# Output product by half tiles in 32-token column tiles, with its queue neighbours in other steps

## The chip, the cores and the metric

One Trainium2 chip, and of it one core. Its engines run side by side, each with its own queue: PE (TensorE: matmuls, with PEld as its loads of weights), DVE (VectorE), ACT (ScalarE), POOL (GpSimd), and SP (SyncE), from which most transfers are issued. The metric is the time of one execution in device microseconds; the median of three executions is given, and lower is better.

## What is computed

Four blocks in a row, each added to `x` (4 batches, 1024 tokens, 256 channels): an attention to a context of 77 rows, a choice of experts, a second attention to that context with 16 heads, and a last attention of the tokens to themselves. Only the last one is touched. Its layer norm, its class of tokens and its output are, cut down:

```python
qkv = (x @ W_qkv).reshape(Bx, Nx, 3, H, D)           # 16 heads of 16
logits = jnp.einsum('bqhd,bkhd->bhqk', q * scale, k)
def masked_attn(tok_mask):                           # the 5 registers are always keys
    l = jnp.where(key_mask[:, None, None, :], logits, -jnp.inf)
    a = jax.nn.softmax(l, axis=-1)
    return jnp.einsum('bhqk,bkhd->bqhd', a, v)
x_pos, x_neg = masked_attn(pos), masked_attn(~pos)
reg_out = (x_pos[:, :REG] + x_neg[:, :REG]) * 0.5
tok_out = jnp.where(pos[:, :, None, None], x_pos[:, REG:], x_neg[:, REG:])
out = jnp.concatenate([reg_out, tok_out], axis=1).reshape(Bx, Nx, Cx) @ W_proj + b_proj
```

So each token attends to the keys of its own class and to the registers, and a register is the mean of two attentions. The output product with `W_proj` (256 x 256) follows, times a gate, added to `x`.

## The kernel before

Up to about 440 us the first three blocks run, in an order that a planner with costs and due times makes (`Plan`). They leave queries, keys and values in device memory (`q_d`, `k_d`, `v_d`). Nothing of that is touched.

The last block is one loop over steps k from -11 to 256 (lines 1902 to 1927). Sixteen steps are a unit: one batch b and four of its heads (u = 4b + g); four units, 64 steps, are a batch. Within a unit a step is one half of the queries (512) and one tile of 128 keys.

- `scores` (L1681): four matmuls of 64 x 128 by 512 columns, one for each head, and after each its exponential on ACT (L1692) into `p`.
- `maxima` (L1640): for a unit that is 11 steps ahead, four matmuls (L1649) and after each a maximum over 512 keys on DVE (L1656), interleaved with the scores head by head.
- `weigh` (L1696): for the step before, four column-tiled matmuls (L1702; 32 output rows for each head, the first of them the sum of the weights), a copy on ACT (L1716 or L1719) and a sum on POOL (L1720). At the end of a unit the sums and the results are laid out anew by transfers (L1726, L1730) into `sums` and `outs`.
- `maxima_end` (L1658) turns the maxima of half a unit (a minimum of negated values on DVE, L1663; a transpose, L1666; two DVE instructions, L1668 and L1669) and copies them by four transfers of 4 KB (L1672) into rows of the queries' tile, so that the scores come out with the maximum subtracted. Scores from step 16u + 8c on need the copies for (u, c).

All matmul outputs share 8 banks in turn (`bank`).

Other work is written as generators, and `plan` (L1859) says by hand in which steps a generator goes on: a number means after `weigh` of that step, a tuple means in the middle of the step (here behind the second head, L1915). The generators that the change touches, with k = 64b:

- `registers` (L1560): masked copies of the register queries on POOL; scores of all 16 heads' registers in four quarters of 256 keys, eight accumulating matmuls each (L1578), each quarter copied by ACT (L1586) in the middle of the next step into `p_r`, a tile that shares two buffers with the divisors; then a maximum, an exponential, transposes (L1600), the product with the values (L1607), and the result `reg_out`. Steps k+14 to k+31.
- `finish` (L1732): a batch's reciprocals (two halves, L1736), their store to device memory (L1738) and two broadcast loads of 512 KB as divisors (L1741), products on POOL (L1744), then for eight tiles of 128 tokens two matmuls by 256 columns (L1755) in one step, gate and sum on DVE (L1757) in the middle of the next, and for every second tile a transfer of `x` to the output. Steps k+67 to k+120, so beside the next batch; the last batch has `finish_unit` (L1766) and `first_heads` (L1783) for its first heads in place of it.
- `biased` (L1840) adds the bias on POOL, `unit` (L1846) loads queries and keys of a unit.

Who follows whom on PE, DVE, ACT and POOL in this loop is the order of the program. For SP it is not: the framework orders the transfers by a plan of its own, in which a transfer that is ready early can pass one that stands ahead of it in the program.

Of the kernel before, what the change touches and what calls it, by code (L numbers as in the profile page):

```python
# [10 lines left out]
F32 = mybir.dt.float32  # L11
# [8 lines left out]
P = 128  # L20
# [139 lines left out]
def block_kernel(ctx: ExitStack, tc: tile.TileContext, t_in: dict, out: bass.AP):  # L160
# [1399 lines left out]
    def registers(b):  # L1560

        qr = QR[b % 2]
        for g in range(G):
            for i in range(2):
                of_pair = qr[:, g, i, 32 * g : 32 * g + J * REG].rearrange("p (h i r) -> p h i r", h=2, i=2)
                q = of_pair[:, :, i, :]
                gp.tensor_tensor(q, bc(QT[(b * G + g) % SLOTS][:, i, 0:REG].bitcast(F32), 1, 2), rmul, ALU.mult)
                gp.tensor_tensor(q, q.bitcast(F32), radd, ALU.add)
            if g % 2:
                yield  # L1570

        p = work.tile([P, S], F32, name="p_r", tag="rinv", bufs=2)
        n = CH // 2
        for h in range(4):
            ps = bank("ps_rs", [P, n])
            for k in range(2 * G):
                g, i = divmod(k, 2)
                pe.matmul(  # L1578
                    ps,
                    qr[:, g, i, :],  # L1580
                    KT[(b * G + g) % SLOTS][:, i, h * n : h * n + n],
                    start=k == 0,
                    stop=k == 2 * G - 1,
                )
            yield
            se.copy(p[:, h * n : h * n + n], ps)  # L1586
            yield
        nm = work.tile([P, 1], F32, name="nm_r")
        ve.tensor_reduce(nm, p, AX.X, ALU.max, negate=True)
        yield  # L1590
        den = work.tile([P, 1], F32, name="den_r")
        se.activation(p, p, AF.Exp, bias=nm, accum_out=den)
        yield
        ve.reciprocal(den, den)
        pt = work.tile([P, T, P], F32, name="pt_r", tag="pt_r", bufs=1)
        for t4 in range(2):
            ps = bank("ps_rt", [P, T // 2, P])
            for i in range(T // 2):
                t = t4 * T // 2 + i
                pe.transpose(ps[:, i, :], p[:, t * P : t * P + P], ident)  # L1600
            se.copy(pt[:, t4 * T // 2 : (t4 + 1) * T // 2, :], ps)
            yield
        ps = bank("ps_ra", [P, J, D])
        for t in range(T):
            for g in range(G):
                r = slice(32 * g, 32 * g + 32)
                pe.matmul(  # L1607
                    ps[r],
                    pt[:, t, r],
                    V[b % 2][:, t, g * J : g * J + J, 1 : 1 + D],  # L1610
                    start=t == 0,
                    stop=t == T - 1,
                )
        mine = work.tile([P, J, D], F32, name="mine_r", bufs=1)
        ve.scalar_tensor_tensor(
            mine.rearrange("p j d -> p (j d)"),
            ps.rearrange("p j d -> p (j d)"),
            den,
            own.rearrange("p j d -> p (j d)"),
            ALU.mult,  # L1620
            ALU.mult,
        )
        yield
        ps = bank("ps_ro", [P, 2, REG])
        for g in range(G):
            at = 64 * (g % 2)
            pe.matmul(
                ps[at : at + 64, g // 2, :],
                mine.rearrange("p j d -> p (j d)"),
                half[:, g, :],  # L1630
                start=True,
                stop=True,
            )
        reg_out[b] = work.tile([P, 2, REG], F32, name="o_r")
        ve.tensor_copy(reg_out[b], ps)
        yield
# [21 lines left out]
    def maxima_end(u, c):  # L1658

        n = T // 2  # L1660
        nm = greatest.pop((u, c))
        least = last.tile([P, J, n], F32, name="nm1", bufs=2)
        ve.tensor_tensor(least, nm[:, :, :, 0], nm[:, :, :, 1], ALU.min)  # L1663
        yield
        ps = bank("ps_n", [J * n, P])
        pe.transpose(ps, least.rearrange("p j t -> p (j t)"), ident)  # L1666
        nmt = last.tile([J * n, 2, P], F32R, name="nmt", bufs=2)
        ve.tensor_copy(nmt[:, 0], ps)  # L1668
        ve.tensor_tensor(nmt[:, 1], ps, nmt[:, 0].bitcast(F32), ALU.subtract)  # L1669
        for i in range(2):  # L1670
            for k in range(2):
                nc.sync.dma_start(  # L1672
                    out=QT[u % SLOTS][k:P:64, i, c * CH : c * CH + CH].bitcast(F32),
                    in_=nmt[2 * n * i : 2 * n * (i + 1), k].bitcast(F32),
                )
        yield
# [55 lines left out]
    def finish(b):  # L1732
        o = outs.pop(b)
        for h in range(2):
            half_of = sums[b][:, h * P // 2 : (h + 1) * P // 2]
            ve.reciprocal(half_of, half_of)  # L1736
            yield
        nc.sync.dma_start(out=rinv_d[b].rearrange("h (t n) -> (h t) n", n=P), in_=sums[b])  # L1738
        rinv = [work.tile([P, S], F32, name="rinv", tag="rinv", bufs=2) for e in range(2)]
        for e in range(2):  # L1740
            nc.sync.dma_start(out=rinv[e], in_=bc(rinv_d[b][8 * e : 8 * e + 8], 1, D))  # L1741
        yield
        for e in range(2):
            gp.tensor_tensor(o[:, e, :], o[:, e, :], rinv[e], ALU.mult)  # L1744
            if e == 0:
                yield
        both = o[:, :, 0:REG]
        gp.tensor_scalar(both, both, 0.5, None, ALU.mult)
        gp.tensor_tensor(both, both, reg_out.pop(b), ALU.add)
        yield  # L1750
        x = X[b]
        for t in range(T):
            ps = bank("ps_o", [P, C])
            for e in range(2):
                pe.matmul(ps, o[:, e, t * P : t * P + P], w_proj[:, e, :], start=e == 0, stop=e == 1)  # L1755
            yield
            ve.scalar_tensor_tensor(x[:, t, :], ps, tg[:, 3:4], x[:, t, :], ALU.mult, ALU.add)  # L1757
            yield
            if t % 2:
                at = (t - 1) * P  # L1760
                nc.sync.dma_start(
                    out=out[b, at : at + 2 * P].rearrange("(t p) c -> p t c", p=P), in_=x[:, t - 1 : t + 1, :]
                )
            yield

    def finish_unit(g):  # L1766
        b = B - 1
# [15 lines left out]
    def first_heads():  # L1783
        x, o = X[B - 1], outs[B - 1]
        for t in range(T):
            ps = bank("ps_o", [P, C])
            pe.matmul(ps, o[:, 0, t * P : t * P + P], w_proj[:, 0, :], start=True, stop=True)
            yield
            ve.scalar_tensor_tensor(x[:, t, :], ps, tg[:, 3:4], x[:, t, :], ALU.mult, ALU.add)
            yield  # L1790
# [83 lines left out]
    for b in range(B):  # L1874
        k = 64 * b
        plan([k - 40, k - 38, k - 16, k - 14] if b else [-5, -4, -2, -1], fetch_values(b))
        scored = [filled(k + n) for n in (17, 19, 21, 23)]
        plan([k + 14, k + 15, *chain(*scored), k + 25, k + 26, k + 27, k + 29, k + 30, k + 31], registers(b))
        plan([k + 27, k + 28, k + 35, k + 36], biased(b))
        if b < B - 1:  # L1880
            tiles = chain(*([n, (n + 1,), n + 2] for n in range(k + 64 + 33, k + 64 + 55, 3)))
            plan([k + 67, k + 68, k + 74, k + 78, k + 80, *tiles], finish(b))
        else:
            plan([k + 19, k + 34], finish_unit(0))
            plan([k + 35, k + 39], finish_unit(1))
            plan(chain(*(filled(k + n) for n in (41, 42, 43, 45, 46, 47, 49, 50))), first_heads())
            plan([k + 51, k + 55], finish_unit(2))
    for u in range(1, NU):
        at = {1: -11, 2: -1}.get(u, 16 * u - (42 if u % G else 34))
        plan([at, at + 1, at + 2, at + 3], rows_ := unit(u))  # L1890
        plan({1: [-7, -6], 2: [3, 4]}.get(u, [at + 8, at + 9] if u % G else [at + 4, at + 5]), rows_)
    for u in range(NU):
        for c in range(2):
            at = 16 * u + 8 * c
            plan([at - 4, at - 3], maxima_end(u, c))
    end = 16 * NU
    mid = T // 2
    plan([end - 6, end - 4], divided(0, mid))
# [3 lines left out]
    for k in range(-LEAD, end + 1):  # L1902
# [7 lines left out]
        if um < NU:  # L1910
            for j in range(J):
                if attends:
                    scores(*now[:3], [j], now[3])
                maxima(um, km, [(j + 2) % J])
                if j == 1:  # L1915
                    for gen in middle.pop(k, []):
                        next(gen, None)
        elif attends:
            scores(*now[:3], range(2), now[3])
            for gen in middle.pop(k, []):  # L1920
                next(gen, None)
            scores(*now[:3], range(2, J), now[3])
        if before is not None:
            weigh(*before, um >= NU)
        before = now
# [89 lines left out]
```

## Time and profile before

| | us |
|---|---|
| median of the runs (1225.14 to 1228.18) | 1227.95 |
| the profiled execution, its own time | 1226.41 |
| its span in the trace | 1224.7 |
| first exponential of the loop | 466.8 |
| a unit without other work (599.4 to 639.2) | 39.8 |
| unit 5, with registers (681.8 to 738.6) | 56.8 |
| unit 6, with output tiles (738.6 to 784.6) | 46.0 |
| last maximum read by DVE starts (step 244) | 1187.8 |

The profile's rows name an engine, a line, what is written from what, and a shape. "x4" counts instructions merged in a row; "[0.81 <-PE ps_m L1649]" behind a row is idle time of the engine before it and what ended it. The ends of matmuls are modelled, so the time of a matmul is best read from the start of one to the start of the next. The granted clock of TensorE was 0.976 on average.

### The profile page before, as it was taken

The page shows a single profiled execution, that of the slowest core. Times are in us where ns is not written, and L with a number is a line of the kernel's source. Part 1 is how long each engine was busy: PE and PEld are TensorE (multiplying, and loading weights), DVE is VectorE, ACT ScalarE, POOL GpSimd, SP SyncE. Part 2 cuts the span into 40 slices and gives each one's busy share as a digit, 9 for nine tenths or more (in the row PEclk, how much of TensorE's full clock was granted, in tenths as well). Part 3 has the DMA queues.
Part 4 walks back from the last instruction along what each step waited for, and adds up shares of the span by engine and source line. Part 5 has one row for each costly group of instructions (what it writes and reads, how often), then busy time and mean ns, then how long its engine had stood idle before and what let it go on. Part 6 is the DMA issues. An engine that isn't in the chain of part 4 may idle for free.

```text
span 1224.7 us, 25560 instructions
## 1 busy us (share of the span) xinstructions
PE 1157.0 (94%) x9164; PEld 611.3 (50%) x9164; DVE 999.4 (82%) x2073; ACT 932.1 (76%) x1918; POOL 607.0 (50%) x682
## 2 busy tenths in 40 slices
PE   7999999999999899999999799999799999799898
PEld 5666776777777454344333344433344443244333
DVE  5898786776864489889999699999689899689884
ACT  4766567876566327899999698899699899689676
POOL 6454566667766532545443544343535334446431
PEclk9999999999999989999999899999899999899899
DMA  8000012111122865532334313334231452300011
GB/s 233 23 1 11 24 61 73 46 37 40 54 82 98 234 180 131 79 62 43 64 57 64 79 32 58 74 64 62 51 65 29 68 97 39 68 20 13 26 27 45
DMA packets 58149, 80.08 MB, mean 65 GB/s; under 512 B 15845, under 2 KB 41360, under 8 KB 58022
## 3 DMA queue, kind: packets, MB, share of 16 engines
q1 hardware_dynamic: 56262, 77.10, 28.2%
q8 instruction: 72, 1.18, 0.4%
q10 hardware_dynamic: 1248, 1.10, 0.3%
q0 software_dynamic: 512, 0.25, 0.2%
q14 instruction: 55, 0.45, 0.1%
HBM read 47.39 MB, written 26.07 MB: 60 GB/s over the span
## 4 chain that ended last, share of the span: by engine, by line
PE 75%; DVE 11%; DMA 5%; ACT 4%; POOL 2%; issue 1%; SPq 0%; ACTq 0%; DVEq 0%; POOLq 0%
PE av L1702 20%; PE sc L1684 18%; PE ps_m L1649 8%; DVE nm L1656 5%; PE ps_st L1121 4%; DMA slot<-nmt 3%; PE ps_av L1133 2%; PE ps_o L1199 2%; PE ps_o L1755 2%; PE ps_q L1234 2%; PE ps_xt L781 2%; PE ps_y L990 2%; PE ps_rs L1578 1%; ACT p L1692 1%; PE ps_xb L886 1%
## 5 line engine op out<-in xcount | busy, mean ns | idle before, releaser
L1656 DVE TENSOR_REDUCE nm<-ps_m 128x1 f32<-128x512 f32 x1024 | 627.8, 677 | 70.8 <-PE ps_m L1649 63.9
L1692 ACT ACTIVATE p<-sc 128x512 f32<-128x512 f32 x1024 | 544.1, 655 | 72.6 <-PE ps_m L1649 61.4
L1720 POOL TENSOR_TENSOR raw<-raw,part 128x512 f32<-128x512 f32 x213 | 272.7, 1281 | 376.7 <-ACT part L1719 365.9
L1649 PE MATMUL ps_m<-slot,slot 64*128 64x512 f32 x768 | 287.0, 458 | 0.9
L1702 PE MATMUL av<-p,v 128*32 128x512 f32 x2048 | 279.8, 614 | 1.2
L1684 PE MATMUL sc<-slot,slot 64*128 64x512 f32 x768 | 248.3, 440 | 29.8 <-DMA slot<-nmt 28.7
L1684 PEld LDWEIGHTS sc<-slot,slot 64*128 64x128 f32 x768 | 126.3, 188 | 183.3 <-ACT p L1692 59.2
L1719 ACT COPY part<-av 128x512 f32<-128x512 f32 x213 | 136.7, 642 | 24.3 <-PE av L1702 22.2
L1649 PEld LDWEIGHTS ps_m<-slot,slot 64*128 64x128 f32 x768 | 130.8, 188 | 39.5 <-ACT p L1692 23.6
L1280 POOL TENSOR_TENSOR ss_all<-ss_all,mhalf 128x16 f32<-128x16 f32 x32 | 92.6, 2903 | 12.8 <-DVE ss_all L1251 12.8
L1649 PE MATMUL ps_m<-kt,qt 64*128 64x512 f32 x256 | 91.6, 461 | 2.6 <-DVE stage L671 2.2
L1684 PE MATMUL sc<-qt,kt 64*128 64x512 f32 x256 | 87.8, 442 | 2.6 <-DMA qt<-nmt 1.2
L1702 PEld LDWEIGHTS av<-p,v 128*32 128x32 f32 x2048 | 41.5, 109 | 80.1 <-ACT p L1692 60.6
L1126 ACT ACTIVATE pt<-ps_st 77x512 f32<-77x512 f32 x128 | 64.2, 599 | 20.2 <-PE ps_st L1121 20.2
L1684 PEld LDWEIGHTS sc<-qt,kt 64*128 64x128 f32 x256 | 43.0, 186 | 67.7 <-DVE nm L1656 31.4
L1069 DVE TENSOR_REDUCE nm<-ps_e 128x4 f32<-128x308 f32 x128 | 51.7, 467 | 14.1 <-PE ps_e L1056 14.0
L769 ACT ACTIVATE xnp<-x,shift_all,rstd_all 128x256 f32<-128x256 f32 x96 | 52.0, 605 | 12.3 <-POOL shift_all L748 9.7
L736 DVE BATCH_NORM_STATS2 bn_st<-x 128x6 f32<-128x256 f32 x128 | 51.5, 402 | 2.3 <-DMA x<-in_x 1.8
L1649 PEld LDWEIGHTS ps_m<-kt,qt 64*128 64x128 f32 x256 | 41.5, 187 | 14.8 <-DVE nm L1656 3.4
L238 ACT COPY xt<-ps_xt 128x512 f32<-128x512 f32 (+1 forms) x57 | 31.7, 582 | 13.8 <-PE ps_xt L781 13.3
L746 POOL TENSOR_TENSOR rstd_all<-rstd_all,mhalf 128x2 f32<-128x2 f32 (+3 forms) x46 | 39.5, 858 | 3.8
L745 POOL TENSOR_SCALAR rstd_all<-mv_all 128x2 f32<-128x2 f32 (+3 forms) x46 | 12.1, 263 | 57.7 <-DVE mv_all L737 46.1
(322 smaller groups left out, 1657.8 us busy)
## 6 DMA issues: line engine op xcount, KB each, us to landing
slot<-k_d SPq DMA_DIRECT2D x72, 128.0 KB
slot<-q_d SPq DMA_DIRECT2D x72, 128.0 KB
q_d<-stage SPq DMA_DIRECT2D x32, 256.0 KB
k_d<-stage SPq DMA_DIRECT2D x16, 512.0 KB
v_d<-vs SPq DMA_DIRECT2D x16, 272.0 KB
v<-v_d SPq DMA_DIRECT2D x16, 272.0 KB
x<-in_x SPq DMA_DIRECT2D x8, 512.0 KB
rin<-inv_d SPq DMA_DIRECT2D x32, 128.0 KB
```

The costliest lines, as they stand in the source:

```text
L736: ve.bn_stats(st[:, i, :], X[b][:, t0 + i, :])
L769: se.activation(to[:, i, :], xb[:, t0 + i, :], AF.Identity, bias=shift[:, i : i + 1], scale=rstd[:, i : i + 1],)
L1069: ve.tensor_reduce(g2["nm"][:, i, r], by_head, AX.X, ALU.max, negate=True)
L1126: se.activation(p[:, r], g2["st", c][r], AF.Exp)
L1280: gp.tensor_tensor(ss, ss, mhalf.to_broadcast([P, H]), ALU.pow)
L1649: pe.matmul(ps, QT[u % SLOTS][r, i, t * P : t * P + P], KT[u % SLOTS][r, i, h * CH : h * CH + CH], start=True, stop=True,)
L1656: ve.tensor_reduce(nm[:, 2 * i + j // 2, t % (T // 2), h : h + 1], ps, AX.X, ALU.max, negate=True)
L1684: pe.matmul(ps, KT[u % SLOTS][r, i, t * P : t * P + P], QT[u % SLOTS][r, i, ch * CH : ch * CH + CH], start=True, stop=True,)
L1692: se.activation(p[j], ps, AF.Exp)
L1702: pe.matmul(ps[32 * j : 32 * j + 32, :], V_all[b % 2][:, at : at + 32], p[j], start=True, stop=True)
L1719: se.copy(part, ps)
L1720: gp.tensor_tensor(to, to, part, ALU.add)
```

## The change

Its core, by part:

```diff
 registers:
-        p = work.tile([P, S], F32, name="p_r", tag="rinv", bufs=2)
-        n = CH // 2
-        for h in range(4):
+        p = keep.tile([P, S], F32, name="p_r", tag="w_qkv")
+        n = CH // 4
+        for h in range(8):
 maxima_end:
-        pe.transpose(ps, least.rearrange("p j t -> p (j t)"), ident)
+        pe.matmul(ps, least.rearrange("p j t -> p (j t)"), ident, start=True, stop=True)
+        yield
 finish:
         nc.sync.dma_start(out=rinv_d[b].rearrange("h (t n) -> (h t) n", n=P), in_=sums[b])
+        yield
...
-        for t in range(T):
-            ps = bank("ps_o", [P, C])
+        for n in range(2 * T):
+            t, cols = n // 2, slice(n % 2 * P, n % 2 * P + P)
+            ps = bank("ps_o", [P, P])
             for e in range(2):
-                pe.matmul(ps, o[:, e, t * P : t * P + P], w_proj[:, e, :], start=e == 0, stop=e == 1)
+                for r in range(J):
+                    at = t * P + 32 * r
+                    pe.matmul(
+                        ps[32 * r : 32 * r + 32], o[:, e, at : at + 32], w_proj[:, e, cols], start=e == 0, stop=e == 1
+                    )
             yield
-            ve.scalar_tensor_tensor(x[:, t, :], ps, tg[:, 3:4], x[:, t, :], ALU.mult, ALU.add)
+            part_x = x[:, t, cols]
+            ve.scalar_tensor_tensor(part_x, ps, tg[:, 3:4], part_x, ALU.mult, ALU.add)
             yield
-            if t % 2:
+            if n % 4 == 3:
...
 first_heads:
-            pe.matmul(ps, o[:, 0, t * P : t * P + P], w_proj[:, 0, :], start=True, stop=True)
+            for r in range(J):
+                at = t * P + 32 * r
+                pe.matmul(ps[32 * r : 32 * r + 32], o[:, 0, at : at + 32], w_proj[:, 0, :], start=True, stop=True)
 the steps:
-        scored = [filled(k + n) for n in (17, 19, 21, 23)]
-        plan([k + 14, k + 15, *chain(*scored), k + 25, k + 26, k + 27, k + 29, k + 30, k + 31], registers(b))
+        scored = [filled(k + n) for n in range(16, 32, 2)]
+        plan([k + 13, k + 15, *chain(*scored), k + 33, k + 34, k + 35, k + 37, k + 38, k + 39], registers(b))
-            tiles = chain(*([n, (n + 1,), n + 2] for n in range(k + 64 + 33, k + 64 + 55, 3)))
-            plan([k + 67, k + 68, k + 74, k + 78, k + 80, *tiles], finish(b))
+            tiles = chain(*([n, (n + 1,)] + [n + 2] * (i % 4 == 3) for i, n in enumerate(range(k + 96, k + 128, 2))))
+            plan([k + 67, k + 68, k + 73, k + 78, k + 82, k + 84, *tiles], finish(b))
-            plan([k + 19, k + 34], finish_unit(0))
-            plan([k + 35, k + 39], finish_unit(1))
-            plan(chain(*(filled(k + n) for n in (41, 42, 43, 45, 46, 47, 49, 50))), first_heads())
+            plan([k + 19, k + 41], finish_unit(0))
+            plan([k + 35, k + 42], finish_unit(1))
+            plan(chain(*(filled(n) for n in range(k + 43, k + 59, 2))), first_heads())
-            plan([at - 4, at - 3], maxima_end(u, c))
+            plan([at - 4, at - 3, (at - 2,)], maxima_end(u, c))
 the middle of a step:
-                if j == 1:
+                if j == 0:
                     for gen in middle.pop(k, []):
```

In words: an output tile is made in two halves of 128 columns, each in four column tiles of 32 tokens, one half every second step (k+96 to k+127 instead of k+97 to k+120); the registers' scores come in eight parts of 128 keys instead of four of 256, and end eight steps later; the store of the reciprocals and the load of the divisors are two steps of the plan, k+73 and k+78, instead of one, k+74, and the products follow at k+82 and k+84; the turn of the maxima is a plain matmul, and what follows it waits for the middle of the next step; and the middle of a step comes behind the first head's maximum instead of the second's (after the last maxima, behind the first score). The loads of a unit's queries and keys keep their steps but for the first two units of a later batch: the first from 16u-34..-29 to 16u-31..-23, the second from 16u-42..-33 to 16u-34..-25.

More of the change, by code (lines that the diff above doesn't have):

```diff
@@ L1763, in finish @@
                 )
-            yield
+                yield
     def finish_unit(g):
@@ L1876, in block_kernel @@
         plan([k - 40, k - 38, k - 16, k - 14] if b else [-5, -4, -2, -1], fetch_values(b))
-        scored = [filled(k + n) for n in (17, 19, 21, 23)]
-        plan([k + 14, k + 15, *chain(*scored), k + 25, k + 26, k + 27, k + 29, k + 30, k + 31], registers(b))
+        scored = [filled(k + n) for n in range(16, 32, 2)]
+        plan([k + 13, k + 15, *chain(*scored), k + 33, k + 34, k + 35, k + 37, k + 38, k + 39], registers(b))
         plan([k + 27, k + 28, k + 35, k + 36], biased(b))
         if b < B - 1:
-            tiles = chain(*([n, (n + 1,), n + 2] for n in range(k + 64 + 33, k + 64 + 55, 3)))
-            plan([k + 67, k + 68, k + 74, k + 78, k + 80, *tiles], finish(b))
-        else:
-            plan([k + 19, k + 34], finish_unit(0))
-            plan([k + 35, k + 39], finish_unit(1))
-            plan(chain(*(filled(k + n) for n in (41, 42, 43, 45, 46, 47, 49, 50))), first_heads())
+            tiles = chain(*([n, (n + 1,)] + [n + 2] * (i % 4 == 3) for i, n in enumerate(range(k + 96, k + 128, 2))))
+            plan([k + 67, k + 68, k + 73, k + 78, k + 82, k + 84, *tiles], finish(b))
+        else:
+            plan([k + 19, k + 41], finish_unit(0))
+            plan([k + 35, k + 42], finish_unit(1))
+            plan(chain(*(filled(n) for n in range(k + 43, k + 59, 2))), first_heads())
             plan([k + 51, k + 55], finish_unit(2))
     for u in range(1, NU):
-        at = {1: -11, 2: -1}.get(u, 16 * u - (42 if u % G else 34))
-        plan([at, at + 1, at + 2, at + 3], rows_ := unit(u))
-        plan({1: [-7, -6], 2: [3, 4]}.get(u, [at + 8, at + 9] if u % G else [at + 4, at + 5]), rows_)
+        at = 16 * u
+        if u == 1:
+            steps = [-11, -10, -9, -8, -7, -6]
+        elif u == 2:
+            steps = [-1, 0, 1, 2, 3, 4]
+        elif u % G == 0:
+            steps = [at - 31, at - 30, at - 26, at - 25, at - 24, at - 23]
+        elif u % G == 1:
+            steps = [at - 34, at - 33, at - 32, at - 31, at - 26, at - 25]
+        else:
+            steps = [at - 42, at - 41, at - 40, at - 39, at - 34, at - 33]
+        plan(steps, unit(u))
     for u in range(NU):
@@ L1918, in block_kernel @@
         elif attends:
-            scores(*now[:3], range(2), now[3])
+            scores(*now[:3], [0], now[3])
             for gen in middle.pop(k, []):
                 next(gen, None)
-            scores(*now[:3], range(2, J), now[3])
+            scores(*now[:3], range(1, J), now[3])
         if before is not None:
```

## Prediction

> **What bounds the kernel now.** I read the page first (engines, chain, groups), then the busy times by stretch, the table of waits, and then single places of the trace. Only the last stage is touched, from about 440 us on: 256 steps, four scores with their exponentials each, and beside them four maxima of a later unit.
>
> ```profile
> PE 1157.0 (94%) x9164; PEld 611.3 (50%) x9164; DVE 999.4 (82%) x2073; ACT 932.1 (76%) x1918; POOL 607.0 (50%) x682
> 599.40:639.20 39.80, 39.74 (x262) 15.54 (x258) 39.66 (x71) 39.42 (x82) 17.92 (x14) 1.00 0.39 65
> 681.80:738.60 56.80, 48.25 (x372) 23.07 (x373) 42.20 (x75) 43.32 (x90) 28.45 (x36) 0.94 0.29 61
> 738.60:784.60 46.00, 45.95 (x282) 18.56 (x279) 42.30 (x77) 40.59 (x81) 20.38 (x16) 1.00 0.33 58
> ```
>
> The last three rows are 16 steps (one unit) each: stretch, length, then PE, PEld, DVE, ACT, POOL busy, clock. The first is a unit with no extra work: 39.8 us, DVE and ACT both full. Eleven maxima in a row take 6.65 us from first start to last end, one lasts 0.67, so one follows another every 0.598 us: four are 2.39 us, the step of 2.42. What DVE or ACT gets extra is paid nearly whole. PE shows as full too, but its ends are modelled; it has some 0.25 us of lead, as seen below. The second unit has registers' scores (and something else), the third the output product.
>
> ```profile
> PE sc L1684 <- DMA slot<-nmt: 28.7, 4, 9.2
> 676.77 1.72 SPq L1672 DMA_DIRECT2D slot<-nmt  x3
> 678.59 1.33 SPq L1741 DMA_DIRECT2D rinv<-rinv_d  x2
> 679.97 0.56 SPq L1672 DMA_DIRECT2D slot<-nmt  x1
> 690.11 0.76 PE L1684 MATMUL sc<-slot,slot 64*128 64x512 f32 x1 [8.62 <-DMA slot<-nmt]
> ```
>
> This is the something else. On SP, two loads of divisors (512 KB each) stand between the third and the fourth 4 KB copy of maxima. The fourth, issued at 679.97, arrives behind 1 MB, and the scores that need it start at 690.11. It happens once in each of batches 0, 1 and 2. By the starts of the exponentials those steps last 12.4, 12.5 and 13.0 us against 2.45.
>
> **Part 1: divisors in other steps.** The store of the reciprocals moves from step k+74 to k+73, the loads from k+74 to k+78, and the copies of maxima are issued in k+78 ahead of them. SP's order is not written by hand. If the loads keep their place in program order, all four copies precede them, and the next copies come eight steps (20 us) later, after the 10 us that the loads need. If SP takes the loads as soon as the store has landed, they precede all four copies, and SP, which in this trace idles 11.2 us from the store's issue at 664.53 to 676.77, has them under way by 672 or so and done by 682, when the scores are due. Behind the loads that wait on SP stand the four copies, and for these PE's scores; each way the split between third and fourth goes. The three long steps are 30.5 us above 2.45; I take **-28**, leaving 2.5 for a remainder (bounds -30.5 and -18, four us of lateness each). Late next after the wait is DVE, whose steps are 2.4 to 3.3 us anyway. The products on POOL move from k+78, k+80 to k+82, k+84; they waited 14.2 us for the loads, which then goes, and nothing waits for them before k+96. The loads of the next batch's first two units move with the registers, to k+33..41 and k+46..55; their maxima start at k+53 and k+69, 12 and 14 steps (29 us and more) later, which hides them; a queue that blocked on one would show as (d) below.
>
> **Part 2: output product.** Before, a 256-column tile is:
>
> ```profile
> 742.66 1.13 PE L1755 MATMUL ps_o<-w_proj,o 128*128 128x256 f32 x4
> 743.72 0.18 PEld L1684 LDWEIGHTS sc<-slot,slot 64*128 64x128 f32 x1 [0.33 <-ACT raw L1716]
> 744.28 1.29 DVE L1656 TENSOR_REDUCE nm<-ps_m 128x1 f32<-128x512 f32 x2 [0.81 <-PE ps_m L1649]
> 745.49 0.48 DVE L1757 SCALAR_TENSOR_TENSOR x<-ps_o,tg,x 128x256 f32<-128x256 f32 x1
> 745.88 3.07 DVE L1656 TENSOR_REDUCE nm<-ps_m 128x1 f32<-128x512 f32 x5
> ...
> 555.44 1.08 PE L1607 MATMUL ps_ra<-v,pt_r 128*32 128x64 f32 x64
> ```
>
> PE spends 1.06 us from 742.66 to 743.72. DVE then idles 0.81, so 0.25 was covered by maxima already in banks; one step later DVE pays 0.39 for the sum (745.49 to 745.88). Together 1.20; by the units, (46.0 + 43.2 - 2 x 39.8) / 8 = 1.20, of which I leave 0.03 to other things: 1.17. After, a half is 8 column-tiled matmuls of two passes each, four of them side by side: four passes in turn. The row of ps_ra has 64 such of 64 columns, 16 passes in 1.08 less the 0.17 of its tail: 0.056 each, so 0.11 at 128 columns, a half 0.44, with no change of array form after av, which is tiled the same. 0.44 less the cover of 0.25 is 0.19; the sum over 128 columns is 0.39 - 128 x 1.07 ns = 0.26 (slope from 474 ns at 256 and 749 at 512 columns of the same operation); some 0.04 is won as the bank is emptied one maximum earlier. A half is 0.41, a tile 0.82: 24 x -0.35 = **-8.4**. If nothing is covered, a half is 0.70, a tile 1.40, and this is +5.5; if all is, -15.6. I take the row's cover. For the last batch the first half of heads (8 tiles of 256 columns) goes from about 0.73 to 0.53 (0.44 less 0.25 plus 0.39, less where DVE is free at the end): **-1.6**.
>
> The Trainium skill, TensorEngine Tiling (Array Packing), section PSUM Bottleneck, speaks against this part: tiling quickens TensorE and leaves the emptying of PSUM as it was. Here emptying even grows, 0.52 for 0.39 a tile; by the rule alone part 2 would be about +3 us and the total 1206.
>
> **Part 3: registers' scores by eighths.**
>
> ```profile
> 516.69 0.30 PEld L1578 LDWEIGHTS ps_rs<-kt,qr 128*128 128x128 f32 x2 [0.85 <-POOL raw L1720]
> 517.03 0.86 PE L1578 MATMUL ps_rs<-slot,qr 128*128 128x256 f32 x6
> 517.83 0.18 PEld L1684 LDWEIGHTS sc<-slot,slot 64*128 64x128 f32 x1
> 547.11 0.66 PE L1600 MATMUL ps_rt<-ident,p_r 128*128 128x128 f32 x4
> ```
>
> A quarter of 8 matmuls by 256 columns is 1.13 us (516.69 to 517.83), the starts 115 ns apart. With 128 columns the weights are still 128 x 128, eight times. The nearest row with 128 columns and full weights is the transposes (last line), whose starts are 109 ns apart: eight are 0.87, with 0.15 for first load and change of form 1.02. So the eighth costs PE nearly what the quarter did, and there are twice as many. Less the 0.25 it is 0.77, plus ACT's copy (0.25 at 256 columns, some 0.15 at 128): 0.92, 7.4 a batch. Before: steps 81 to 88 are 24.6 us; less 8 x 2.42 and 0.7 for maxima 4.5. That is 2.8 a batch, **+11** for four. Bounds: if the columns decide (55 ns), an eighth is 0.5 and this is -2; if the matmul falls to the two-pass rate of 128 columns (2 x 107 = 213 ns) it is 256 x 0.1 = 26 more, +37. Other register work moves, no amount changes; p_r's new place is free since the projection of values.
>
> **Part 4: ends of maxima.** A matmul (two passes of 107 ns, no change of form) for the transpose, 0.2 us either way; the two DVE instructions come a maximum later, so DVE no longer idles for the transpose (4.2 us in 7 places). **-2**, bounds -4 and +1. The copies start 0.6 us later: 594.54 plus three of 0.59, the fourth is issued at 596.3, its score starts 599.6, and one without traffic (issued 464.69, score at 466.17 after waiting) lands in 1.5. So 1.8 is free and 0.6 used.
>
> **Part 5: last batch.**
>
> ```profile
> 1131.61 4.49 DVE L1663 TENSOR_TENSOR nm<-nm 128x16 f32<-128x16 f32 x1
> ...
> 1131.11 1.27 POOL L1843 TENSOR_TENSOR x<-x,b_proj 128x512 f32<-128x512 f32 x1
> ...
> 1134.80 1.25 POOL L1720 TENSOR_TENSOR raw<-raw,part 128x512 f32<-128x512 f32 x1
> ```
>
> The median of this DVE operation is 0.175. Here it ends when POOL, behind a 2.36 us product of step 226 and without a gap since 1129.88, falls idle at 1136.05. The change puts that product at 233: **-4** (bounds -4.3, and +2 if the products at 233 and 234 hold the next one, step 236).
>
> The Trainium skill, SBUF - State Buffer, section Who interferes with whom, says that a VectorE instruction with two SBUF inputs contends with GpSimd's reads, the second waiting for the other's whole instruction. One instruction would be 1.27; the row shows several in turn, and the row decides. By the rule this term would be -1 and the total 1197.5.
>
> **Sum.** -28 - 8.4 - 1.6 + 11 - 2 - 4 = -33. The profiled execution took 1226.4 (span 1224.7): 1193.4. The median of the runs is 1.5 higher: **1194.5**.
>
> **Rivals.** (a) *The loads still stand before a copy.* For: SP's order follows a plan that the change doesn't state, and 1 MB takes 10 us. Against: both orders above. Part 1 gives nothing: 1222.5. (b) *Eighths at the two-pass rate*, 213 ns a matmul: +26, 1220.5. For: no such matmul of 128 columns is in the trace. (c) *Products on POOL hold DVE* at k+84, as in the rows of part 5, in three batches, 4.3 each: 1207.5. Against: POOL has product and two sums, 4.9 us, in the two steps ahead, and with eighths these last 5.7, so there is a gap. (d) *Slower:* the copies of maxima, issued behind a later DVE place, come late at every half unit. Place: the first sc of each; price: 31 us for each us of lateness (31 halves). From 1.1 us, that is with copies 2.3 us later than I take, it eats the 33: 1231.7 with 1.2. Against: 1.2 us of margin, SP idle there.
>
> **Chances.** Forecast 0.64, (a) 0.09, (b) 0.10, (c) 0.08, (d) 0.09. A measurement of this kernel tells 0.3% (3.7 us) from no change. (a) with eighths some 5 us dearer gives 0.04 for no difference, taken from (a) and (b); the rest of these, (c) and the forecast are faster, 0.87; (d) is slower, 0.09. The range goes from 1177 (part 2 at its best, part 3 at nothing) to 1222 ((b), and nearly (a)); (d) and some of (a) are left out.
>
> **What would show it.** Right: no wait of sc for nmt above 2 us; units 5, 9, 13 near 49 us instead of 57; the starts of ps_rs 105 to 115 ns apart; DVE idle under 0.3 before each half's step; L1663's longest under 2 us. Wrong: rinv loads still between copies; ps_rs starts 60 or 200 apart; idle DVE of 0.4 or more at each half; PE waiting for nmt in every unit.

## The result and the profile after

| | before | after |
|---|---|---|
| median of the runs beside each other, us | 1228.07 (1225.14 to 1228.23) | 1245.08 (1238.34 to 1248.66) |
| ratio, 95% interval | | 1.0138, 1.009 to 1.0185 |
| profiled execution, its span | 1226.41, 1224.7 | 1238.34, 1236.6 |
| unit 3 (no other work) | 39.8 | 40.5 |
| unit 5, 9, 13 (registers) | 56.8, 57.6, 57.5 | 60.4, 60.9, 60.6 |
| units 6 and 7 (output tiles) | 89.2 | 91.1 |
| unit 14 | 56.6 | 52.9 |

The kernel became 17.0 us slower; the forecast was 33 faster, and the range ended at 1222. Lengths of units and steps here and below are from the start of a first exponential (ACT, line of `p`) to the next such start.

The page's line of engines after; the shares are within two points of those before, and tell nothing of the loss:

```profile
PE 1167.5 (94%) x10044; PEld 639.0 (52%) x10044; DVE 1006.5 (81%) x2097; ACT 943.1 (76%) x1934; POOL 606.0 (49%) x682
```

The busy times of units 3, 5 and 6 after (stretch, length, then PE, PEld, DVE, ACT, POOL busy, granted clock, DMA share, GB/s):

```profile
600.27:640.74 40.47, 40.33 (x264) 16.64 (x260) 40.15 (x71) 39.69 (x82) 17.86 (x14) 1.00 0.47 71
683.60:744.03 60.43, 51.10 (x328) 25.56 (x329) 41.34 (x71) 42.86 (x89) 26.95 (x28) 0.92 0.29 64
744.03:791.26 47.23, 46.92 (x472) 22.03 (x468) 44.12 (x83) 43.32 (x85) 20.41 (x16) 1.00 0.21 45
```

Unit 5 is 60.4 us long, and no engine is busy for more than 51 of them; for 8.2 us (686.95 to 695.10 in the timeline below) none runs at all. The table of waits (engine and line, what it waited for, us in total, times, longest) says that this is another wait than before. That of `sc` for `nmt`, 28.7 us before, is gone as forecast; it is 3.4 in the page's groups. In its place stands 28.7 us of POOL waiting for classes, and PE waiting for POOL:

```profile
PEld ps_rs L1578 <- POOL qr L1568: 31.2, 11, 9.4
POOL qr L1567 <- DMA slot<-cls_d: 28.7, 4, 9.7
PE ps_rs L1578 <- POOL qr L1568: 26.7, 3, 9.3
```

The timeline around step 80 (start, length, engine, line, in brackets the idle time before) shows it:

```profile
680.70 2.27 SPq L1673 DMA_DIRECT2D slot<-nmt  x4
...
683.03 1.27 SPq L1743 DMA_DIRECT2D rinv<-rinv_d  x2
...
684.17 0.47 PE L1685 MATMUL sc<-slot,slot 64*128 64x512 f32 x1 [0.69 <-DMA slot<-nmt]
...
684.34 1.71 SPq L1480 DMA_DIRECT2D slot<-cls_d  x4
...
686.34 0.61 PE L1578 MATMUL ps_rs<-slot,qr 128*128 128x128 f32 x4
695.10 0.20 POOL L1567 TENSOR_TENSOR qr<-slot,rmul 128x10 fp32r<-128x10 f32 x1 [9.07 <-DMA slot<-cls_d]
...
695.64 0.47 PE L1578 MATMUL ps_rs<-slot,qr 128*128 128x128 f32 x1 [8.69 <-POOL qr L1568]
```

SP's order is the one that was forecast: four copies of maxima, then the 1 MB of divisors. But right behind the 1 MB come four transfers of classes (`classes`, L1480) for the batch's fourth unit. They had stood behind the 1 MB in the kernel before as well, behind the fourth copy of maxima:

```profile
680.58 1.39 SPq L1480 DMA_DIRECT2D slot<-cls_d  x4
```

There PE stood until 690.11 for that copy anyway, and no row of its waits is for `slot<-cls_d`. The prediction asked when the loads of the next batch's first two units are needed, and did not look at the fourth unit's classes. Its maxima need them much later, but `registers` reads the first columns of the same tile at once: POOL's product (L1567) waits 9.07 us for the classes, the seventh and eighth matmul of the first eighth wait for POOL, and the scores, which stand behind them in the program, wait too (the next `sc` starts at 696.49). The first eighth is also wanted one step earlier than the first quarter was, in step k+16 instead of k+17.

### The profile page after: what moved, and what is told of

Same layout as the page of the kernel before. It is cut to its first block, busy times and chain, and to the rows that moved or that the text cites. A ratio compares the mean times of both kernels' runs of the same rounds, so it can differ in the third digit from the quotient of the medians.

```text
span 1236.6 us, 27407 instructions
## 1 busy us (share of the span) xinstructions
PE 1167.5 (94%) x10044; PEld 639.0 (52%) x10044; DVE 1006.5 (81%) x2097; ACT 943.1 (76%) x1934; POOL 606.0 (49%) x682
## 4 chain that ended last, share of the span: by engine, by line
PE 67%; DVE 15%; DMA 6%; ACT 5%; POOL 3%; issue 2%; SPq 2%; ACTq 0%; POOLq 0%; DVEq 0%
PE av L1703 17%; PE sc L1685 14%; PE ps_m L1649 8%; DVE nm L1656 8%; PE ps_st L1121 4%; DMA slot<-cls_d 3%; PE ps_rs L1578 3%; ACT p L1693 3%; PE ps_av L1133 2%; PE ps_o L1199 2%; PE ps_q L1234 2%; PE ps_xt L781 2%; PE ps_o L1760 2%; PE ps_y L990 1%; DVE bn_st L736 1%
## 5 line engine op out<-in xcount | busy, mean ns | idle before, releaser
L1656 DVE TENSOR_REDUCE nm<-ps_m 128x1 f32<-128x512 f32 x1024 | 634.4, 679 | 84.2 <-PE ps_m L1649 56.3
L1649 PE MATMUL ps_m<-slot,slot 64*128 64x512 f32 x768 | 282.5, 454 | 1.3
L1685 PE MATMUL sc<-slot,slot 64*128 64x512 f32 x768 | 236.0, 430 | 4.4 <-DMA slot<-nmt 3.4
L1649 PEld LDWEIGHTS ps_m<-slot,slot 64*128 64x128 f32 x768 | 129.6, 187 | 50.1 <-ACT p L1693 37.7
L1720 ACT COPY part<-av 128x512 f32<-128x512 f32 x213 | 132.3, 621 | 23.1 <-PE av L1703 21.7
L1685 PEld LDWEIGHTS sc<-qt,kt 64*128 64x128 f32 x256 | 43.1, 186 | 67.6 <-DVE nm L1656 30.4
L1578 PE MATMUL ps_rs<-slot,qr 128*128 128x128 f32 x192 | 29.1, 281 | 26.8 <-POOL qr L1568 26.7
```

The lines of the kernel that those rows point to most:

```text
L1578: pe.matmul(ps, qr[:, g, i, :], KT[(b * G + g) % SLOTS][:, i, h * n : h * n + n], start=k == 0, stop=k == 2 * G - 1,)
L1649: pe.matmul(ps, QT[u % SLOTS][r, i, t * P : t * P + P], KT[u % SLOTS][r, i, h * CH : h * CH + CH], start=True, stop=True,)
L1656: ve.tensor_reduce(nm[:, 2 * i + j // 2, t % (T // 2), h : h + 1], ps, AX.X, ALU.max, negate=True)
L1685: pe.matmul(ps, KT[u % SLOTS][r, i, t * P : t * P + P], QT[u % SLOTS][r, i, ch * CH : ch * CH + CH], start=True, stop=True,)
L1720: se.copy(part, ps)
```

## The experiments

Each difference below is to the kernel before as run beside it (medians 1228.07, 1225.83, 1227.83, 1226.79 in the four groups of runs). "From unit 2" is the time from that unit's first exponential to the end of the trace: the first exponential of all comes between 463.8 and 470.3 us, after work that no edit touches, so this column tells small effects better than one span does. The first batch's registers, in units 0 and 1, are not in it.

| kernel | median | to before | ratio, 95% interval | from unit 2 |
|---|---|---|---|---|
| before | | 0 | | 665.2 |
| changed kernel | 1245.08 | +17.0 | 1.009 to 1.0185 | 679.6 |
| 1 before, divisors moved | 1218.68 | -7.2 | 0.9897 to 0.9948 | 650.4 |
| 2 before, classes moved | 1232.07 | +6.2 | 1.0033 to 1.0071 | 667.7 |
| 3 before, both ("calm base") | 1197.68 | -28.2 | 0.9734 to 0.9793 | 634.1 |
| 4 changed kernel, classes moved | 1215.53 | -10.3 | 0.9867 to 0.9936 | 647.0 |
| 5 calm base, ends of maxima | 1209.90 | -17.9 | 0.9837 to 0.9893 | 644.8 |
| 6 calm base, output tiles | 1192.44 | -35.4 | 0.9689 to 0.9753 | 627.4 |
| 7 calm base, last batch's steps | 1192.67 | -35.2 | 0.9689 to 0.9760 | 628.0 |
| 8 as 7, with eighths | 1213.30 | -14.5 | 0.9863 to 0.9922 | 646.3 |
| 9 calm base, matmul for transpose | 1202.54 | -24.3 | 0.9781 to 0.9821 | 636.0 |
| 10 calm base, bank emptied late | 1205.00 | -21.8 | 0.9797 to 0.9850 | 640.9 |
| 11 calm base, middle after one head | 1196.41 | -30.4 | 0.9728 to 0.9774 | 634.3 |
| 12 calm base, 6 and 7 together | 1188.60 | -38.2 | 0.9671 to 0.9705 | 623.9 |

An interval reaches some 2 to 6 us to each side; differences under that are not leaned on alone.

### 1 to 4: what stands behind the 1 MB

**1. Divisors moved, in the kernel before:**

```diff
-        p = work.tile([P, S], F32, name="p_r", tag="rinv", bufs=2)
+        p = keep.tile([P, S], F32, name="p_r", tag="w_qkv")
...
         nc.sync.dma_start(out=rinv_d[b]..., in_=sums[b])
+        yield
-            plan([k + 67, k + 68, k + 74, k + 78, k + 80, *tiles], finish(b))
+            plan([k + 67, k + 68, k + 73, k + 78, k + 82, k + 84, *tiles], finish(b))
```

> Kernel before with part 1 alone, as the change has it: store of the divisors at k+73, loads at k+78 behind the four copies of maxima, products on POOL at k+82 and k+84, the registers' probabilities in the other buffer. Theory (the wait is handed on): the four transfers of classes of the batch's fourth unit now stand behind the 1 MB; POOL's rounding of the registers' queries waits some 9 us for them, the registers' scores for POOL, PE for these. So the three stalls stay, one step later (steps k+17 instead of k+16): 1228 within 4. Rival (the prediction's part 1 by itself is right and the loss in the changed kernel comes from the other parts alone): 28 less, 1200. Second rival (the loads' own traffic is what stops PE, wherever they stand in the queue): 1228 as well, but then the next two kernels don't gain either.

Measured: 7.2 less. The wait is handed on as the theory says, but it is shorter than it expected (1228 within 4 was missed): the waits now read

```profile
POOL qr L1567 <- DMA slot<-cls_d: 19.2, 3, 6.5
...
PE ps_rs L1578 <- POOL qr L1568: 14.6, 3, 5.0
```

POOL comes to the product 4.4 us after the first transfer of classes was issued, where it is 1.7 in the changed kernel, so less of the transfers' time is left to wait for, and the three long steps are 9.2 to 9.5 us instead of 12.4 to 13.0. That is 9.5 less in units 5, 9 and 13. (This profiled execution, 1209.3, is the fastest of seven, the others took 1215.8 to 1219.3; in it the long step 229 of the last batch, 6.5 us before, took 2.9. More of that under 7.)

**2. Classes moved, in the kernel before:** those of each batch's fourth unit are issued at k+73 instead of k+78 and k+79.

```diff
-        plan({1: [-7, -6], 2: [3, 4]}.get(u, [at + 8, at + 9] if u % G else [at + 4, at + 5]), rows_)
+        late = [at + 3, at + 3] if u % G == G - 1 else [at + 8, at + 9]
+        plan({1: [-7, -6], 2: [3, 4]}.get(u, late if u % G else [at + 4, at + 5]), rows_)
```

> Kernel before with one edit: the classes of each batch's fourth unit are issued at k+73, ahead of the divisors' store, instead of k+78 and k+79. Theory: the fourth copy of maxima still stands behind the loads, so PE waits as before: 1228 within 4, the wait of sc for nmt unchanged at about 9 us in three places. Rival (classes alone were the cause all along): 1200.

Measured: 6.2 more, a little worse than the 4 allowed. The fourth copy of maxima still stands behind the loads; the long steps are 13.2, 14.6 and 12.3 us. Why it is slower, and not the same, stays open. One edit alone gives a part, the other alone nothing.

**3. Both:**

> Kernel before with both edits: divisors loaded behind the copies of maxima, and the classes of the fourth unit issued ahead of the store, so that nothing of the next 15 us stands behind the 1 MB. Theory: the three steps of 12.4 to 13.0 us fall to about 2.5 to 3.5, 28 to 30 us in all, and PE's windows of half clock behind them go as well: 1198 (1194 to 1203). Rival (traffic itself, or a third transfer behind the loads): 1215 or more, with a new wait of about the same length in the table of waits.

Measured: 28.2 less, 1197.68 where 1198 was expected. The queue and the unit in the trace:

```profile
668.81 3.24 SPq L1480 DMA_DIRECT2D slot<-cls_d  x4
680.37 2.29 SPq L1672 DMA_DIRECT2D slot<-nmt  x4
682.71 1.27 SPq L1742 DMA_DIRECT2D rinv<-rinv_d  x2
```
```profile
685.34:732.30 46.96, 46.70 (x370) 22.39 (x369) 42.03 (x75) 43.17 (x89) 27.57 (x33) 1.00 0.36 72
```

The same 1 MB moves in the same place, unit 5 is 47.0 instead of 56.8, and the granted clock 1.00 instead of 0.94. So it isn't the traffic that stops PE, but what is queued behind it: the second rival of experiment 1 falls. Two loads of values (`v<-v_d`, from 684.02) still stand behind the 1 MB here, and no row of the waits names them: what counts is how soon the tile is read.

**4. The changed kernel with the classes moved** (`steps = [at - 42, at - 41, at - 40, at - 39, at - 39, at - 39]` where `u % G == G - 1`):

> Changed kernel with one edit: the classes of each batch's fourth unit are issued at k+73, ahead of the divisors' store. Theory: its three stalls of 13.7 to 14.3 us (with 4.1 in the step behind) go, 30 to 34 us: 1210 (1204 to 1216). What is left of the gap to the other kernel with both edits, some 12 us, are the changed kernel's other parts together (ends of maxima and eighths against tiles and last batch). Rival (another wait behind the loads): 1235 or more.

Measured: 10.3 below before, so 27.3 less than the changed kernel. Unit 5 is 49.6, with the clock at 1.00 where it was 0.92:

```profile
694.36:743.95 49.59, 48.98 (x328) 24.64 (x329) 41.37 (x71) 42.63 (x89) 26.96 (x28) 1.00 0.36 76
```

One branch of the plan that the change does not have is worth 27 us. What is left, 17.9 between experiments 3 and 4, is the price of all the other parts together. 5 to 8 take it apart.

### 5 to 8: the other parts, one by one

**5. Ends of maxima** (matmul for the transpose, the second `yield` of `maxima_end`, the place `(at - 2,)`, the middle of a step after one head):

> The kernel with both loads and classes moved (1197.7, called the calm base below), with part 4 added: matmul for the transpose, the two DVE instructions behind the next step's first maxima, and the place in the middle of a step after one head instead of two. Theory (ends cost time): in the changed kernel's unit 3, which has no other extra work, each end costs some 0.35 more; 31 ends are 10: 1207 (1203 to 1210). Prediction's part 4: 2 less, 1196. Rival (the extra step length seen in unit 3 is only the tail of its neighbours): 1198 within 2.

Measured: 10.2 more than the calm base (12.2 by the medians as they stand). The theory holds. Who waited for whom around the bank of this small product, in the calm base and then in this kernel (what waited: us, times):

```profile
  DVE nmt L1668: 4.2, 7
  PEld sc L1684: 1.4, 6
```
```profile
  PEld av L1703: 4.1, 17
  PEld sc L1685: 2.5, 3
```

DVE's 4.2 us of waiting for the transpose are gone, as forecast. What came instead is PE waiting for these DVE instructions, 17 times 0.24 us; whether that is the price, experiments 9 to 11 ask. In unit 3 each half unit's last step, the one behind an end, is 2.8 us where it was 2.4.

**6. Output tiles** (halves, column tiles, steps 96 to 127; and `first_heads` in column tiles):

> Calm base with part 2 alone: output product by halves of 128 columns in column tiles of 32 tokens, two steps a half, and the last batch's first product in column tiles. Theory (as read from the changed kernel: a pair of halves at 1.06 to 1.18 against 1.20 to 1.29): 4 to 7 less, 1192. Prediction's part 2: 10 less, 1187.7. The page's rule that emptying of PSUM decides: 3 more, 1201.

Measured: 7.2 less than the calm base; units 6 and 7 are 87.7 instead of 89.1. Halves without column tiles were not tried, so the run does not tell the two edits of this part apart.

**7. Last batch's steps** (`finish_unit` 0 and 1 end at k+41 and k+42, `first_heads` every second step from k+43):

> Calm base with part 5 alone: second places of finish_unit 0 and 1 at k+41 and k+42, first products every second step from k+43. Theory (prediction's part 5: the held instruction of step 229 goes): 4 less, 1193.7. Rival (the hold only moves: steps 235 and 236 of the changed kernel are 5.5 and 4.4 us): 1198 within 2.

Measured: 7.0 less. The DVE group of the held instruction (busy, mean ns) in the calm base and here:

```profile
L1663 DVE TENSOR_TENSOR nm<-nm 128x16 f32<-128x16 f32 x32 | 13.7, 428 | 1.0
```
```profile
L1663 DVE TENSOR_TENSOR nm<-nm 128x16 f32<-128x16 f32 x32 | 9.5, 297 | 1.0
```

The 4.2 us that the one instruction was held are gone, and unit 14 is 50.1 instead of 56.3. Step 235 is longer in return (4.9 for 3.4), which the rival had as eating all of it. In experiment 1 the same step was short as well, with that part of the program as before: how long the hold lasts depends on how POOL and DVE happen to lie to each other. That POOL is what holds it is argued from the two ends in the prediction's rows, 1136.10 and 1136.05.

**8. Registers by eighths**, on top of 7, since `finish_unit(0)` must come behind the registers' new end:

> Calm base with part 5 and part 3: registers' scores by eighths over sixteen steps, the registers' later places and the units' loads with them. Theory (prediction's part 3, 2.8 a batch): 11 more than part 5 alone. Rival (the eighths are paid by columns): 2 less than part 5 alone. If the four parts don't add up to the 17.8 between the calm base and the changed kernel with the classes moved, they cost each other something.

Measured: 20.6 more than 7, not 11. An eighth in the timeline:

```profile
699.30 0.44 PE L1578 MATMUL ps_rs<-kt,qr 128*128 128x128 f32 x2
...
699.57 0.83 PE L1578 MATMUL ps_rs<-slot,qr 128*128 128x128 f32 x6
...
700.34 0.50 PE L1684 MATMUL sc<-slot,slot 64*128 64x512 f32 x1
...
701.85 0.27 ACT L1586 COPY p_r<-ps_rs 128x128 f32<-128x128 f32 x1
```

From 699.30 to 700.34 are 1.04 us: eight matmuls of 128 columns cost PE nearly as much as eight of 256 (1.13 in the prediction's rows); forecast 1.02. A pair of steps with an eighth is 3.22 to 3.23 and 2.69 to 2.75 instead of twice 2.44 (steps 82, 88 and 90; in the others lies other work too): 0.79 for PE and 0.25 to 0.31 for the copy, some 1.07 in all, where 0.92 was forecast. The rest sits in the first pair, 4.1 and 2.7, and in the step ahead of it, 2.7 for 2.4. SP's own waits in this kernel have a row that is not in experiment 7:

```profile
SPq L1672 <- POOL qr L1567: 8.6, 3, 2.9
```

The copies of maxima for step 80 go into rows of a tile that the registers' first products read. Before, these products stood behind the copies (k+14 against k+13). Now they are issued in k+13 ahead of them, and SP waits for POOL, up to 2.9 us in three batches; the copies go out 2.8 us ahead of their step instead of 5.0. The move was not tried by itself, but in experiment 4, whose plan has it too, the second score of step 80 waits for just these copies:

```profile
694.95 0.46 PE L1685 MATMUL sc<-slot,slot 64*128 64x512 f32 x1 [0.69 <-DMA slot<-nmt]
```

That is most of the 0.9 us by which step 80 is longer than the other first steps of a pair.

The four parts sum to 10.2 - 7.2 - 7.0 + 20.6 = +16.6; together (4 less 3) they were +17.9. The 1.3 between them is within the noise.

### 9 to 11: what in the ends of maxima costs

**9. Matmul alone:**

> Calm base with one line of part 4: a matmul with the identity in place of the transpose of the maxima. Part 4 as a whole cost 12.2 (1209.9). Theory A (the later place costs): 1198 within 2. Theory B (the matmul costs, two passes of 107 ns and its own form): 31 ends at 0.3 or more, 1207.

**10. Later place alone** (transpose kept, a `yield` behind it, `(at - 2,)`):

> Calm base with the other half of part 4: transpose kept, the two DVE instructions that empty its bank in the middle of the next step (here after two heads, where the middle is in this kernel). Theory A (the bank stays taken while PE should fill it again; 31 ends at 0.3 to 0.4): 1207 to 1211. Theory B (the matmul, or the middle's move): 1198 within 2. The prediction's own reason (DVE no longer idles for the transpose): 1196.

**11. Middle of a step after one head alone:**

> Calm base with only the middle of a step moved, from behind the second head to behind the first; in this kernel it empties banks of the registers' scores and of the output product. Prediction: some 0.04 a bank won, 24 tiles and 16 quarters, 1 to 2 less, 1196. Rival (DVE or ACT then meets the bank before PE has filled it, 0.2 each): 1206. Theory A of the ends says nothing here; if this costs 5 or more, it has a share in part 4's 12.2.

Measured against the calm base: the matmul +3.9 (between theories A and B, outside both), the later place +6.4 (a little under A's bound), the middle -2.2 (as the prediction, and within the noise: from unit 2 on it is +0.2). The three sum to 8.1, the whole was 10.2; the noise covers the 2.1 between them.

The matmul costs only where PE has other work (unit 5: 47.5 for 47.0; unit 3: nothing), and its size is less sure: +1.9 from unit 2 on. DVE waits 6.8 us for its result in 11 places, where it waited 4.2 in 7 for the transpose.

With the later place alone, the last step of each half of unit 3, where nothing else goes on, is 2.75 long instead of 2.39. The weight loads at the end of step 55, in the calm base and then in experiment 10:

```profile
620.47 0.18 PEld L1684 LDWEIGHTS sc<-slot,slot 64*128 64x128 f32 x1 [0.30 <-ACT part L1719]
620.47 0.18 PEld L1649 LDWEIGHTS ps_m<-kt,qt 64*128 64x128 f32 x1
620.97 0.16 PEld L1702 LDWEIGHTS av<-p,v 128*32 128x32 f32 x8 [0.31 <-ACT p L1692]
```
```profile
620.39 0.18 PEld L1685 LDWEIGHTS sc<-slot,slot 64*128 64x128 f32 x1 [0.30 <-ACT part L1720]
620.89 0.18 PEld L1649 LDWEIGHTS ps_m<-kt,qt 64*128 64x128 f32 x1 [0.32 <-ACT p L1693]
621.31 0.16 PEld L1703 LDWEIGHTS av<-p,v 128*32 128x32 f32 x8 [0.24 <-DVE nm L1656]
```

From the last score to `av` are 0.92 us instead of 0.50. The matmul of the maxima now waits for an exponential, of which it uses nothing, so by the code it can only be waiting for its bank; experiment 5 has the same two waits there. In experiment 10 no `av` waits for `nmt`: the 17 waits of experiment 5 are not what the later place costs. That a bank given back later changes the order in which the 8 come round is argued, not shown. That DVE is spared a wait, the prediction's reason for the ends, shows in no time.

### 12: what is worth keeping

> Calm base with parts 2 and 5, without parts 3 and 4: what the single runs say is worth keeping. If they add up, 1197.7 less 5.2 and 5.0: 1187.5. If part 2's last-batch share and part 5 buy the same time (both touch the first product of the last batch): 1190. Rival (tiles and the later products of POOL hold each other up): 1193 or more.

Measured: 1188.60, 38.2 less than before, ratio 0.9688 (0.9671 to 0.9705): the sum of the parts (28.2 + 7.2 + 7.0 = 42.4) less 4.2. Of these 2.5 lie in units 14 and 15, which 6 and 7 both shorten: 107.3 us in the calm base, 104.1 and 101.3 with one of them, 100.6 with both. It beats the kernel before and the changed one, and has from the change the divisors' steps, the output product and the last batch, with the classes moved, which the change does not do.

## Why the prediction was wrong, step by step

**Part 1, -28: the step that failed.** Its mechanism and size were right (experiment 3: -28.2) for a queue in which nothing behind the loads is wanted soon. SP's order came as the first of its two cases: all four copies, then the loads. For that case it says "the next copies come eight steps (20 us) later, after the 10 us that the loads need", as if the next copies were the next transfer that anyone waits for. Between them stand the classes, 1.3 us behind the loads, and POOL reads their tile at once: 9.07 us of waiting at step 80, 28.7 in four places. "Late next after the wait is DVE" failed with it: next was POOL, and behind it PE. In the changed kernel the part gave back 27.3 of its 28 (experiment 4). The sign that was to show it right, no wait of `sc` for `nmt` above 2 us, came true (1.4 at most) in a kernel that was slower: it names the old wait, not one that takes its place.

**Part 4, -2: wrong in sign, +10.2.** The wait it removes was real (4.2 us in 7 places, gone), but its removal shows in no time. The price was looked for in DVE's instructions, which did not change in number, and in the copies' lateness. The rows of step 55 show it in PE instead, whose matmuls wait for banks; how much of the 10.2 goes that way was not measured.

**Part 3, +11: right in mechanism, short by 9.6.** The term for PE was right (1.04 measured, 1.02 forecast, cover 0.25 as taken). The copy on ACT was put at 0.15 and cost 0.25 to 0.31, 0.28 in the middle: 8 x 4 x 0.13 = 4.2. The move of the registers' products from k+14 to k+13, past the copies of maxima, was counted as nothing ("no amount changes"): 0.9 in each first pair, 3.6, and 0.3 in the step ahead, 1.2 (the wait of 0.69 for the copies explains most of the first). The last 0.6 is not placed.

**Part 2, -8.4 and -1.6: right in sign, -7.2 in all, for another reason.** A half in the changed kernel:

```profile
745.57 0.62 PE L1760 MATMUL ps_o<-w_proj,o 128*32 128x128 f32 x16
...
746.12 0.50 PE L1685 MATMUL sc<-slot,slot 64*128 64x512 f32 x1
...
746.69 0.69 DVE L1656 TENSOR_REDUCE nm<-ps_m 128x1 f32<-128x512 f32 x1 [0.28 <-PE ps_m L1649]
747.30 0.34 DVE L1765 SCALAR_TENSOR_TENSOR x<-ps_o,tg,x 128x128 f32<-128x128 f32 x1
747.55 1.88 DVE L1656 TENSOR_REDUCE nm<-ps_m 128x1 f32<-128x512 f32 x3
```

PE spends 0.55 from 745.57 to the next score, not 0.44, so a tile of two halves costs it 1.10, no less than the 1.06 before. The cover, the part of PE's stretch that maxima already in banks hide from DVE, is 0.27 here (0.55 less DVE's idle 0.28), about the 0.25 taken, and the sum on DVE 0.25 (747.30 to 747.55), as worked out. By this sum a tile wins because the cover counts twice, once for each half. A half is 0.53 here and not 0.41, a tile some 1.06 against 1.20; in experiment 6, units 6 to 8 are 1.8 us shorter than in the calm base, 0.22 a tile where 0.35 was forecast. The Trainium skill, TensorEngine Tiling (Array Packing), section PSUM Bottleneck, says that tiling leaves the emptying as it was. The emptying did grow, 0.50 a tile for 0.39; by that alone the part would have been about +3 (the prediction's estimate), and the measurement decides: PE's stretch and its cover counted too.

**Part 5, -4: right in mechanism, -7.0 alone, beyond its bound of -4.3.** The hold went (the longest L1663 of the changed kernel is 1.04 us); a part of it came back in the changed kernel as the wait of the first product for POOL's work with the divisors (L1785 to L1788), where steps 235 and 236 are 5.5 and 4.4:

```profile
1170.87 0.64 PE L1797 MATMUL ps_o<-w_proj,o 128*32 128x256 f32 x8 [2.22 <-POOL o L1788]
```

**Rivals.** (a), loads still ahead of a copy, did not happen. (b), the two-pass rate, did not: the starts lie 0.11 apart. (c) was not seen. (d), the slower one, had the copies of maxima late at every half unit, and they were not: `sc` waits for `nmt` 3.4 us in 4 places in the whole kernel. The case that happened, another transfer behind the loads that is read at once, was not among the rivals at all.

**The sum.** From -33 to +17.0 are 50.0 us: 27.3 classes behind the loads, -0.2 the rest of part 1, 12.2 ends of maxima, 9.6 registers, 2.8 tiles and first product, -3.0 last batch; these are 48.7, and the 1.3 by which the parts cost more together than alone makes 50.0. Two slips in the recorded sums change nothing of this: SP stands for 11.9 us from the store's end (664.87) to 676.77, not 11.2, and 1193.4 with 1.5 is 1194.9, not 1194.5.

## What to carry to other kernels

When a large transfer is moved in a queue, list everything that will be issued in the time that it takes *after* the move, and for each the first reader of the tile that it writes, whatever it is loaded for. A wait that another wait hides shows in no table of waits before; the queue's rows do show the transfer, and the code who reads its tile first. And an idle row of the engine that empties banks is no gain by itself: here the later emptying that was to spare it cost 6.4 us.

## What the runs showed that was not expected

- A stop of PE for some 9 us costs more than itself: the granted clock over unit 5 is 0.92 with the stop and 1.00 without, and the step behind it is 4.1 us against 2.7.
- Four small transfers issued 1.3 us behind 1 MB were waited for until 10.8 us after their issue (684.34 to 695.10); issued ahead of it (experiments 2 to 4), no row of the waits names their tile's readers as waiting for them.
- The DVE instruction of step 229 (L1663) is held 4.49 us in the calm base and under 1 in the profiled execution of experiment 1, with the same instructions around it on DVE and POOL: the stretch in which POOL works without a gap lies a little differently against it.
